# Half of the window-attention products on GpSimd, in chunks of 1024 elements, in a fused attention and expert kernel

## The chip, the cores and the metric

The kernel runs on one core of a Trainium2 chip. A core has five engines with queues of their own: TensorE (PE in the profile, its weight loads PEld), VectorE (DVE), ScalarE (ACT), GpSimd (POOL) and SyncE (SP). Each executes its queue strictly in the order in which the kernel was built, and engines wait for each other by semaphores. The metric is the time of one execution on the device in microseconds (us), as the median of several runs.

## The reference

The input x is 2 x 1024 rows of 256 numbers. Its rows are normalized (xn), and the result is the sum of three things:

```
x + attention(xn) + experts(xn)

attention: each row is 16 tokens of 16 channels; qkv = tok @ qkv_w
  two branches of 8 channels: windows of 8 tokens along one axis, then along the other
  softmax(q * 8**-0.5 @ k.T) @ v + depthwise 3x3 convolution of v within the window
  concatenate, project, layer norm, add to tok, transpose back
experts: 16 experts of 176 units, each row takes 6 of them, chosen in 2 of 4 groups
  sum over the 6 of weight * (silu(xn @ gate.T) * (xn @ up.T)) @ down.T, and one shared expert
```

The change concerns only the middle of the attention: for each window of 8 tokens and 8 channels, 8 x 8 scores as sums over 8 products q * k, and 8 x 8 outputs as sums over 8 products of a softmax weight and v.

## The kernel before, in words

The kernel first normalizes the rows, computes the shared expert, and sorts the rows by which experts they need. From about 108 us on, a long loop (lines 983 to 1015) does the routed experts on TensorE and lays the attention in between.

The expert work goes in slots: 96 of the kind "six" and 26 of the kind "extra", two to a pair. Per slot, `up` (line 827) makes a gate and an up product on TensorE (L831, four matmul records), ScalarE applies silu (L833), and VectorE multiplies gate, weight and up product to one hidden product (L834, `hms`; called h below). Per pair, TensorE transposes the hidden products (L845), ScalarE copies them out (L847), and TensorE multiplies by the down weights (L857, or L865 for extras). For extras VectorE adds each result to its tile (L920, called y); for sixes, once per tile of 128 rows (L912, called Y). A finished tile is added to the output by an indirect DMA that GpSimd issues (L926, "adds"). All rows of a tile were fetched by indirect DMAs of GpSimd (L802, "gathers") before.

The attention is done four times, for each half of the batch and each half of the columns, by `attention(b, h)` (line 642). One attention has 16 groups of windows, 8 for each branch, each with 8 windows' worth of work in the free dimension:

- `gather` and `project(i)`, i from 0 to 7: TensorE multiplies by the q, k and v weights (L660) and ScalarE copies q and k (L662, L663) and v (L664, L665) into place.
- `products(n)` and `scores(n)`, n from 0 to 12 in steps of NW = 4: VectorE multiplies 2048 elements on each of 128 partitions (L673) and sums them in eights (L677).
- `highest` (L683, L684, called X, and the exponential on ScalarE, L685) and `totals` (L688, L689, called S).
- `weighted(n)` and `values(n)`: the same with the weights and v (L694, L699).
- `divide` (L707, called D), and `transposed` back by TensorE (L714, L716).

The products of one chunk are in the room tagged "prod", 2048 elements per partition, which the next chunk takes again. After the four attentions, `attended` projects and normalizes the result, with some multiplies and adds on GpSimd (L782, L787), and GpSimd issues the DMAs that add it to the output (L954).

What sets the order: each step of the attention carries an estimated cost on VectorE and on TensorE, by hand. The loop over the slots adds up both and gives out the next attention step while VectorE's sum is below `pace` times TensorE's (line 1000), so that the steps are spread over the slots and end when 66 us of TensorE's work are left (`END`). The scheduler of the language then builds the queue of each engine from that, and may put a ready instruction ahead of one that it takes to be ready later.

Of the kernel before, what the change touches and what calls it, by code (L numbers as in the profile page):

```python
# [8 lines left out]
F32 = mybir.dt.float32  # L9
# [4 lines left out]
ALU = mybir.AluOpType  # L14
# [8 lines left out]
P = 128  # L23
B, H, W = 2, 1024, 256
C = 16
HD = 8
WIN = 8
NW = 4
E, I = 16, 176
LAST = I - P  # L30
HALF = P // 2
# [18 lines left out]
def csw_block_moe(ctx: ExitStack, tc: tile.TileContext, x, qkv_w, conv_w0, conv_b0, conv_w1, conv_b1,  # L50
# [19 lines left out]
    nc = tc.nc  # L70
# [3 lines left out]
    work = ctx.enter_context(tc.tile_pool(name="work", bufs=1))  # L74
# [74 lines left out]
    for c in range(16):  # L149
        n = sum(P // 2 if k % 2 == 0 else P for k in range(c)) + (((16 - c) * P - 1) / 2 if c % 2 == 0 else 0)  # L150
# [185 lines left out]
    full = [P, 16, E]  # L336
# [114 lines left out]
    for c in range(15, -1, -1):  # L451
        n = 16 - c
# [186 lines left out]

    oT = big.tile([P, 4, 2, 4, P], F32, name="oT", tag="oT")  # L640

    def attention(b, h):
        steps = []

        qk = work.tile([P, 2, 2, 8, WIN, HD], F32, tag="qk", name=f"qk{b}{h}")
        v = work.tile([P, 2, 8, HD, WIN], F32, tag="v", name=f"v{b}{h}")
        s = work.tile([P, 16, WIN, WIN], F32, tag="f1024", name=f"s{b}{h}", bufs=3)
        o = work.tile([P, 16, WIN, HD], F32, tag="f1024", name=f"o{b}{h}", bufs=3)
        sums = small.tile([P, 16, WIN], F32, name=f"sums{b}{h}", tag="sums")
        rows = work.tile([P, 8, P], F32, tag="f1024", name=f"rows{b}{h}", bufs=3)  # L650
        full = [P, NW, WIN, WIN, HD]

        def gather():
            for i in range(2):
                nc.scalar.copy(rows[:, 4 * i : 4 * i + 4].rearrange("p i (w r) -> p i w r", r=4),
                               xnT[:, h, :, 64 * b : 64 * b + 64].rearrange("p (i r) (w u) -> p u i w r", r=4, u=2)[:, i])

        def project(i):
            pq = ps_m.tile([P, 3, 8, C], F32, tag="m", name="pq")
            nc.tensor.matmul(pq.rearrange("p s t c -> p (s t c)"), lhsT=rows[:, i],  # L660
                             rhs=wq.rearrange("p s t c -> p (s t c)"), start=True, stop=True)
            nc.scalar.copy(qk[:, :, 0, i], pq[:, 0:2, :, 0:HD])  # L662
            nc.scalar.copy(qk[:, :, 1, :, i], pq[:, 0:2, :, HD:C])  # L663
            nc.scalar.copy(v[:, 0, i], pq[:, 2, :, 0:HD].rearrange("p t c -> p c t"))  # L664
            nc.scalar.copy(v[:, 1, :, :, i], pq[:, 2, :, HD:C])  # L665

        held = {}

        def products(n):
            pr = work.tile([P, NW, WIN, WIN, HD], F32, tag="prod", name="pr")  # L670
            br, m = n // 8, n % 8
            q_, k_ = (qk[:, part, br, m : m + NW] for part in range(2))
            nc.vector.tensor_tensor(pr, q_.unsqueeze(3).to_broadcast(full), k_.unsqueeze(2).to_broadcast(full), ALU.mult)  # L673
            held[n] = pr

        def scores(n):
            nc.vector.tensor_reduce(out=s[:, n : n + NW], in_=held.pop(n), axis=AX.X, op=ALU.add)  # L677

        rows_s = s.rearrange("p n q k -> p (n q) k")

        def highest():
            top = small.tile([P, P], F32, tag="top", name="top", bufs=1)
            nc.vector.tensor_reduce(out=top, in_=rows_s, axis=AX.X, op=ALU.max)  # L683
            nc.vector.tensor_tensor(rows_s, rows_s, top.unsqueeze(2).to_broadcast([P, P, WIN]), ALU.subtract)  # L684
            nc.scalar.activation(rows_s, rows_s, AF.Exp, scale=HD**-0.5)  # L685

        def totals():
            nc.vector.tensor_reduce(out=sums.rearrange("p n q -> p (n q)"), in_=rows_s, axis=AX.X, op=ALU.add)  # L688
            nc.vector.reciprocal(sums, sums)  # L689

        def weighted(n):
            pr = work.tile([P, NW, WIN, HD, WIN], F32, tag="prod", name="pv")
            br, m = n // 8, n % 8
            nc.vector.tensor_tensor(pr, s[:, n : n + NW].unsqueeze(3).to_broadcast(full),  # L694
                                    v[:, br, m : m + NW].unsqueeze(2).to_broadcast(full), ALU.mult)
            held[n] = pr

        def values(n):
            nc.vector.tensor_reduce(out=o[:, n : n + NW], in_=held.pop(n), axis=AX.X, op=ALU.add)  # L699

        def divide():
            xo = held["xo"] = work.tile([P, 8, 8, C], F32, tag="xo", name=f"xo{b}{h}")
            for br in range(2):
                to = xo[:, :, :, HD * br : HD * br + HD]
                if br:
                    to = to.rearrange("p i t c -> p t i c")
                nc.vector.tensor_tensor(to, o[:, 8 * br : 8 * br + 8],  # L707
                                        sums[:, 8 * br : 8 * br + 8, :].unsqueeze(3).to_broadcast([P, 8, WIN, HD]),
                                        ALU.mult)

        def transposed(i):
            po = ps_m.tile([P, 4, P], F32, tag="m", name="po")
            for j in range(4):
                nc.tensor.transpose(po[:, j, :], held["xo"][:, i + j].rearrange("p t c -> p (t c)"), ident)  # L714
            to = oT.rearrange("p g h r (b w i) -> p g h b i w r", b=B, i=2)[:, :, h, b, i // 4]
            nc.scalar.copy(to, po.rearrange("p j (w r) -> p j w r", r=4))  # L716


        steps.append((0.3, 0.0, gather))
        for i in range(8):  # L720
            steps.append((0.3, 0.65, lambda i=i: project(i)))
        for n in range(0, 16, NW):
            steps.append((2.3, 0.0, lambda n=n: products(n)))
            steps.append((2.3, 0.0, lambda n=n: scores(n)))
        steps.append((2.5, 0.0, highest))
        for n in range(0, 16, NW):
            steps.append((2.3, 0.0, lambda n=n: weighted(n)))
            if n == 0:
                steps.append((1.5, 0.0, totals))
            steps.append((2.3, 0.0, lambda n=n: values(n)))  # L730
        steps.append((1.4, 0.0, divide))
        for i in (0, 4):
            steps.append((0.3, 0.5, lambda i=i: transposed(i)))
        return steps

# [194 lines left out]
    att = []  # L930

    def all_steps():
        for steps in (extras_listed(), weights_prepared()):
            for _ in steps:
                yield 1.0, 0.1, lambda: None
        yield from attention_steps()

    def attention_steps():
        for b in range(B):
            for h in range(2):  # L940
                yield from attention(b, h)
        xe = []
        yield 0.6, 0.0, lambda: xe.extend(edges())
        att.extend(work.tile([P, 8, W], F32, tag=tag, name="att") for tag in ("prod", "qk"))
        for g in range(4):
            for h in range(2):
                yield 1.4, 3.9, lambda: attended(g, h, xe, att)
            if g % 2:
                waiting.extend([lambda m=m, b=b, n=g // 2: attention_added(m, b, n) for m in range(2) for b in range(B)])

    def attention_added(m, b, n):

        cols = slice(P * n, P * n + P)
        nc.gpsimd.dma_start(out=out[b, 512 * m : 512 * m + 512, cols].rearrange("(c p) d -> p c d", p=64),  # L954
                            in_=att[m][64 * b : 64 * b + 64, :, cols], accum_op=ALU.add)
# [2 lines left out]
    of_slot = {"six": (0.5, 2.0), "extra": (1.4, 2.25)}  # L958
    of_tile = (1.05, 0.25)
    END = 66  # L960
    in_walk = [11 * 1.0 + 4 * (16 * 2.3 + 3.3 + 2.5 + 1.5 + 1.4) + 0.6 + 8 * 1.4, 11 * 0.1 + 4 * 6.2 + 8 * 3.9]
    done = [0.0, 0.0]
    whole = [in_walk[n] + NTL * TOPK * of_slot["six"][n] + NX * of_slot["extra"][n] + NTL * of_tile[n] for n in range(2)]
    pace = (whole[0] - END * of_slot["six"][0] / of_slot["six"][1]) / (whole[1] - END)
# [18 lines left out]
    for u in range(len(laid_out) + 2):  # L983
        for q in range(2):
# [102 lines left out]
```

## Time and profile before

| what | value |
|---|---|
| median of 3 runs | 469.24 us (465.8 to 472.79) |
| the profiled execution | 463.79 us, its span 462.1 us |
| granted TensorE clock, mean | 0.987 |
| from 137.3 to 370.2 us | the four attentions, between pairs of expert slots |
| from 370.2 to 444 us | the rest of the expert slots with the end of the attention |
| from 444 to the end | the last tiles' adds to the output |

The four attentions, from the first product's start to the end of the last division, stand in VectorE's timeline at 137.32 to 185.73, 199.75 to 253.9, 266.61 to 315.1 and 321.39 to 370.2 us.

How to read the profile: a group's line has the source line, engine, operation, output and inputs with their shapes, the count, the busy time and the mean of one in ns, and then how long the engine was idle just before and what ended that. A timeline's line has start and duration in us, and in brackets the idle time ahead and what it waited for. A table of windows has start and end, length, and the busy time of each engine with its number of instructions.

### The profile page before, as it was taken

How to read it: one execution, taken by the hardware profiler on the slowest of the kernel's cores; microseconds unless marked ns; L12 is line 12 of the kernel's file. 1: busy time of each engine (PE TensorE's matmuls, PEld its weight loads, DVE VectorE, ACT ScalarE, POOL GpSimd, SP SyncE). 2: the span in 40 equal slices, each digit the busy share in tenths (PEclk: the TensorE clock that was granted, in tenths of full speed). 3: DMA queues.
4: the chain of work that ended last, by engine and by line, in shares of the span. 5: the costliest groups of instructions: out<-in, count | busy, mean ns of one | idle time of the engine just before them, and what ended most of it. 6: DMA issues, size and time to landing. Idle time of an engine off the chain costs nothing.

```text
span 462.1 us, 6437 instructions
## 1 busy us (share of the span) xinstructions
PE 412.7 (89%) x1726; PEld 258.8 (56%) x1727; DVE 304.3 (66%) x555; ACT 214.3 (46%) x510; POOL 108.4 (23%) x127
## 2 busy tenths in 40 slices
PE   0999999996999998999999999998998899999980
PEld 0436566463666665555556666665666545556760
DVE  5326956745729999469999199995999933333220
ACT  2936167222354463463632453626343147777220
POOL 7300000425400000000001312120221026766821
PEclk9999999998999999999999999999999999999996
DMA  8999960413310000100001221201013110185552
GB/s 234 325 287 279 260 211 2 106 39 86 96 31 21 24 27 24 28 5 27 20 24 35 47 41 35 43 24 27 23 35 84 35 17 19 48 123 99 75 72 23
DMA packets 38323, 35.39 MB, mean 77 GB/s; under 512 B 4112, under 2 KB 36208, under 8 KB 38256
## 3 DMA queue, kind: packets, MB, share of 16 engines
q1 hardware_dynamic: 28336, 23.28, 17.8%
q0 software_dynamic: 8896, 10.65, 14.3%
q10 hardware_dynamic: 1056, 1.05, 0.7%
q8 instruction: 16, 0.26, 0.2%
q14 instruction: 19, 0.16, 0.1%
HBM read 26.44 MB, written 10.62 MB: 80 GB/s over the span
## 4 chain that ended last, share of the span: by engine, by line
PE 39%; DVE 35%; issue 9%; ACT 7%; DMA 6%; DVEq 1%; POOL 1%; POOLq 0%; SPq 0%; ACTq 0%
PE pr_u L831 10%; DVE pr L673 6%; PE pp L766 6%; DVE s L677 6%; DVE pv L694 5%; DVE o L699 5%; PE pr_y L857 5%; DVE hms L834 4%; PE pg L270 3%; PE py L285 2%; PE pq L660 2%; DMA xg<-xw_d,of 2%; PE pu L270 2%; DMA xx<-in_x_dram 2%; PE plT L252 2%
## 5 line engine op out<-in xcount | busy, mean ns | idle before, releaser
L831 PE MATMUL pr_u<-w1s,xsT 128*128 x384 | 127.9, 464 | 0.7 <-DVE hms L834 0.4
L833 ACT ACTIVATE sg<-pr_u 128x176 f32<-128x176 f32 x122 | 38.6, 318 | 134.4 <-PE pr_u L831 107.4
L831 PEld LDWEIGHTS pr_u<-w1s,xsT 128*128 128x128 f32 x384 | 71.5, 191 | 35.9 <-issue 5.5
L926 POOL DMA_INDIRECT out_dram<-ysum,of x16 | 31.6, 1975 | 225.6 <-ACT sg L833 124.5
L834 DVE SCALAR_TENSOR_TENSOR hms<-sg,w,pr_u 128x176 f32<-128x176 f32 x96 | 36.8, 391 | 35.2 <-ACT sg L833 35.2
L673 DVE TENSOR_TENSOR pr<-qk 128x2048 f32<-128x2048 f32 x16 | 36.6, 2287 | 20.0 <-ACT qk L662 19.7
L845 PE MATMUL ph<-ident,hms 128*128 128x128 f32 x183 | 33.8, 280 | 8.7 <-DVE hms L834 7.3
L845 PEld LDWEIGHTS ph<-ident,hms 128*128 128x128 f32 x183 | 23.4, 142 | 29.7 <-DVE hms L834 13.2
L694 DVE TENSOR_TENSOR pv<-s,v 128x2048 f32<-128x2048 f32 x16 | 36.6, 2286 | 2.4 <-ACT s L685 2.4
L677 DVE TENSOR_REDUCE s<-pr 128x256 f32<-128x2048 f32 x16 | 36.5, 2278 | 0.0
L699 DVE TENSOR_REDUCE o<-pv 128x256 f32<-128x2048 f32 x16 | 36.3, 2268 | 0.0
L831 PE MATMUL pr_u<-w1s,xd 128*128 x104 | 33.5, 460 | 0.0
L847 ACT COPY hT<-ph 128x384 f32<-128x384 f32 x61 | 29.2, 478 | 3.1 <-PE ph L845 1.5
L857 PE MATMUL pr_y<-w2a,hT 128*128 x96 | 28.7, 380 | 0.0
L857 PE MATMUL pr_y<-w2b,hT 112*128 x96 | 28.7, 379 | 0.0
L857 PE MATMUL pr_y<-wts,hT 128*128 128x256 f32 x96 | 28.5, 379 | 0.0
L660 PE MATMUL pq<-wq,rows 128*128 128x384 f32 x64 | 24.7, 502 | 2.7 <-ACT oT L716 2.1
L285 PE MATMUL py<-room 128*128 128x256 f32 x96 | 23.9, 387 | 1.4 <-DVE room L279 1.4
L831 PEld LDWEIGHTS pr_u<-w1s,xd 128*128 128x128 f32 x104 | 19.6, 189 | 9.3 <-issue 0.4
L270 PE MATMUL pg<-xnT,room 128*128 128x512 f32 x48 | 24.1, 614 | 0.0
L270 PE MATMUL pu<-xnT,room 128*128 128x512 f32 x48 | 23.0, 602 | 0.0
L285 PEld LDWEIGHTS py<-room 128*128 128x128 f32 x96 | 17.4, 190 | 6.7 <-DVE room L279 2.5
(320 smaller groups left out, 635.3 us busy)
## 6 DMA issues: line engine op xcount, KB each, us to landing
w1s<-in_w_dram SPq DMA_DIRECT2D x22, 256.0 KB, 5.3
wts<-in_w_dram SPq DMA_DIRECT2D x61, 64.0 KB, 2.1
wts<-in_w_dram SPq DMA_DIRECT2D x61, 48.0 KB, 1.7
xw_d<-xx SPq DMA_DIRECT2D x4, 544.0 KB, 9.5
w2a<-in_w_dram SPq DMA_DIRECT2D x4, 512.0 KB, 10.5
out_dram<-ysh POOLq DMA_DIRECT2D x4, 512.0 KB, 5.5
xr<-xw_d POOLq DMA_DIRECT2D x4, 512.0 KB, 4.9
out_dram<-att POOLq DMA_DIRECT2D x8, 256.0 KB, 7.0
```

The costliest lines, as they stand in the source:

```text
L270: nc.tensor.matmul(ps, lhsT=w1h[:, half, h, P * m : P * m + P], rhs=xnT[:, h, 4 * k : 4 * k + 4, :].rearrange("p l q -> p (l q)"), start=( ...
L285: nc.tensor.matmul(py, lhsT=hms[k, m][:, P * c : P * c + P], rhs=w2h[:, m], start=(m == 0), stop=(m == 2))
L660: nc.tensor.matmul(pq.rearrange("p s t c -> p (s t c)"), lhsT=rows[:, i], rhs=wq.rearrange("p s t c -> p (s t c)"), start=True, stop=True)
L673: nc.vector.tensor_tensor(pr, q_.unsqueeze(3).to_broadcast(full), k_.unsqueeze(2).to_broadcast(full), ALU.mult)
L677: nc.vector.tensor_reduce(out=s[:, n : n + NW], in_=held.pop(n), axis=AX.X, op=ALU.add)
L694: nc.vector.tensor_tensor(pr, s[:, n : n + NW].unsqueeze(3).to_broadcast(full), v[:, br, m : m + NW].unsqueeze(2).to_broadcast(full), ALU. ...
L699: nc.vector.tensor_reduce(out=o[:, n : n + NW], in_=held.pop(n), axis=AX.X, op=ALU.add)
L831: nc.tensor.matmul(pu, lhsT=lhs[:, h, :], rhs=w1s[:, :, h, bass.ds(e * I, I)], start=(h == 0), stop=(h == 1))
L833: nc.scalar.activation(sg, pu[:, 0, :], AF.Silu)
L834: nc.vector.scalar_tensor_tensor(hm[:, 0:I], sg, w, pu[:, 1, :], op0=ALU.mult, op1=ALU.mult)
L845: nc.tensor.transpose(ph[:, s, :], units[:, P * s : P * s + P], ident)
L857: nc.tensor.matmul(py, lhsT=l_, rhs=r_, start=start and n == 0, stop=stop and n == 2)
```

## The change

Chunks have 2 groups of windows (NW = 2, 1024 elements), so there are eight chunks to the scores and eight to the values. The room for products is one tile of two halves that is kept for all four attentions. Chunks 1, 3, 5 and 7 are multiplied by GpSimd in the second half, the others by VectorE in the first; all sums stay on VectorE. GpSimd's first product is issued ahead of VectorE's first, and each later one right behind the sum that has read its half. `totals` comes ahead of all the weighted products. The estimated costs are 1.25 for each product of VectorE and each sum, nothing for a product of GpSimd; `in_walk`, from which `pace` follows, is made to match. One of the two tiles in which `attended` collects its result, which took the room of the products after the last attention, now is that kept tile.

```diff
-NW = 4
+NW = 2
...
+    prods_ = []
+    def multiplier(n):
+        return nc.gpsimd if n // NW % 2 else nc.vector
     def attention(b, h):
         steps = []
+        if not prods_:
+            prods_.append(work.tile([P, 2, NW, WIN, WIN, HD], F32, tag="prod", name="prods"))
+        prods = prods_[0]
...
         def products(n):
-            pr = work.tile([P, NW, WIN, WIN, HD], F32, tag="prod", name="pr")
+            pr = prods[:, n // NW % 2]
             br, m = n // 8, n % 8
             q_, k_ = (qk[:, part, br, m : m + NW] for part in range(2))
-            nc.vector.tensor_tensor(pr, q_.unsqueeze(3).to_broadcast(full), k_.unsqueeze(2).to_broadcast(full), ALU.mult)
+            multiplier(n).tensor_tensor(pr, q_.unsqueeze(3).to_broadcast(full), k_.unsqueeze(2).to_broadcast(full), ALU.mult)
...
         def weighted(n):
-            pr = work.tile([P, NW, WIN, HD, WIN], F32, tag="prod", name="pv")
+            pr = prods[:, n // NW % 2]
...
-            nc.vector.tensor_tensor(pr, s[:, n : n + NW].unsqueeze(3).to_broadcast(full),
+            multiplier(n).tensor_tensor(pr, s[:, n : n + NW].unsqueeze(3).to_broadcast(full),
...
-        for n in range(0, 16, NW):
-            steps.append((2.3, 0.0, lambda n=n: products(n)))
-            steps.append((2.3, 0.0, lambda n=n: scores(n)))
+        def in_turn(product, total):
+            steps.append((0.0, 0.0, lambda: product(NW)))
+            for n in range(0, 16, 2 * NW):
+                steps.append((1.25, 0.0, lambda n=n: product(n)))
+                steps.append((1.25, 0.0, lambda n=n: total(n)))
+                def last(n=n):
+                    total(n + NW)
+                    if n + 3 * NW < 16:
+                        product(n + 3 * NW)
+                steps.append((1.25, 0.0, last))
+        in_turn(products, scores)
         steps.append((2.5, 0.0, highest))
-        for n in range(0, 16, NW):
-            steps.append((2.3, 0.0, lambda n=n: weighted(n)))
-            if n == 0:
-                steps.append((1.5, 0.0, totals))
-            steps.append((2.3, 0.0, lambda n=n: values(n)))
+        steps.append((1.3 + 0.95, 0.0, totals))
+        in_turn(weighted, values)
...
-    in_walk = [11 * 1.0 + 4 * (16 * 2.3 + 3.3 + 2.5 + 1.5 + 1.4) + 0.6 + 8 * 1.4, 11 * 0.1 + 4 * 6.2 + 8 * 3.9]
+    in_walk = [11 * 1.0 + 4 * (24 * 1.25 + 3.3 + 2.5 + 2.25 + 1.4) + 0.6 + 8 * 1.4, 11 * 0.1 + 4 * 6.2 + 8 * 3.9]
```

The queue of VectorE as built, from the first attention's first product on, one letter for each instruction. P and W are products of VectorE (scores, values), T and V the sums of them, t and v the sums of GpSimd's products, X, S and D as above, h a hidden product, y and Y additions to a tile, e the edges and a the end of the attention; a bar stands behind each attention's last D and ahead of the next one's first P.

```
before
PThPhThPhThPhThXhXhWhShSVhWhhVhWhVhWhVhWhyVyhDhD | yyhhyyhhyy |
PhTPhyTyhhPyTyhhPyhThyXyXhyyWhhSVhyhyShWyVyhhWyVyhhWyhVhDD | hhhhYh |
PhTPhThPhThYPhThXhXhWhhSYSVhhWhVhWhVhYWhVhDD | hh |
PhTPhTYhPhThPhThhXYXhWhShSVhWhhYVhWhVhWhVhhDD |
YeeheeaaahaaaahaaahaaahaaaYhaaahaaahaahhhhYhhhhhhYhhY

after
PTtPhTtPhTthPthThXXhSWhhSVhvWhVhvWvhVhWvVhDhD | hhyyhhyyhhyyhhyyhhyy |
PThtPTPhytyThthPyTythXhyXySyShhyWhVhyvyWhVhvyWyVhvhyWyVhvhDyD | yhhhhhhYhhh |
PThtPTtPhThtYPthThXXhSWhhSVhvYWhVhvWvhVhWvhVDhD | Yhhhh |
PThtPTPhtYThthPtThXhXSWhhYShVhvWvhVhWvhVvhYWDhVhD |
eehhhhYeehaaaahaaahaaahaaahaaaYhaaahaaahaahhhhYhhhhhhYhhY
```

The queue of GpSimd after the change has, in this order: all 16 gathers; 16 products of the first two attentions; five adds; the third attention's four score products, an add, two weighted products, an add, two weighted products; an add; the fourth attention's three score products, an add, the fourth score product, a weighted product, an add and the fetch of the first rows for `attended` (L758), three weighted products; and then what was there before.

More of the change, by code (lines that the diff above doesn't have):

```diff
@@ L943, in attention_steps @@
         yield 0.6, 0.0, lambda: xe.extend(edges())
-        att.extend(work.tile([P, 8, W], F32, tag=tag, name="att") for tag in ("prod", "qk"))
+        att.extend([prods_[0].rearrange("p a w q k d -> p (a w q k d)").rearrange("p (n d) -> p n d", d=W),
+                                       work.tile([P, 8, W], F32, tag="qk", name="att")])
         for g in range(4):
```

## The prediction

> **What bounds the kernel now.** I read the busy shares first, then the stages as windows, then the groups by line, then the timeline of single instructions. TensorE leads the span, but TensorE's busy time is modelled from pipelined matmuls, so a stage has to say which engine ends last.
>
> ```profile
> PE 412.7 (89%) x1726; PEld 258.8 (56%) x1727; DVE 304.3 (66%) x555; ACT 214.3 (46%) x510; POOL 108.4 (23%) x127
> ```
>
> The windows of the third attention (266 to 314), the pause behind it, the fourth (321 to 370) and the tail of expert work; columns are window, length, and busy time of each engine with its instructions:
>
> ```profile
> core 0: us, PE busy (x) PEld busy (x) DVE busy (x) ACT busy (x) POOL busy (x), PEclk, DMA share, GB/s
> 266.00:314.00 48.00, 44.88 (x182) 30.65 (x180) 46.47 (x43) 19.84 (x58) 10.09 (x5) 1.00 0.20 38
> 314.00:321.00 7.00, 6.25 (x27) 4.20 (x28) 1.82 (x4) 4.75 (x16) 0.00 (x0) 1.00 0.09 22
> 321.00:370.00 49.00, 44.34 (x179) 30.10 (x177) 47.70 (x45) 18.00 (x54) 9.36 (x5) 1.00 0.19 43
> 421.00:444.00 23.00, 23.00 (x99) 16.66 (x98) 6.56 (x16) 9.63 (x23) 13.47 (x13) 1.00 0.69 110
> ```
>
> VectorE is full inside an attention (47.70 of 49) and almost idle between two (1.82 of 7), where TensorE is. The timeline of TensorE in the tail gives the price of expert work when nothing holds it: one pair of slots every 4.00 us, so 2.0 us per hidden product (h, L834).
>
> ```profile
> 425.35 2.53 PE L831 MATMUL pr_u<-w1s,xsT 128*128 x8
> 429.35 2.53 PE L831 MATMUL pr_u<-w1s,xsT 128*128 x8
> ```
>
> The prices on VectorE and GpSimd by line:
>
> ```profile
> L673 DVE TENSOR_TENSOR pr<-qk 128x2048 f32<-128x2048 f32 x16 | 36.6, 2287 | 20.0 <-ACT qk L662 19.7
> L677 DVE TENSOR_REDUCE s<-pr 128x256 f32<-128x2048 f32 x16 | 36.5, 2278 | 0.0
> L782 POOL TENSOR_TENSOR a<-a,lw 128x512 f32<-128x512 f32 x6 | 8.3, 1386 | 12.1 <-DVE a L781 12.1
> L787 POOL TENSOR_TENSOR att<-a,xr 128x256 f32<-128x256 f32 x12 | 12.6, 1074 | 5.3 <-DMA xr<-xw_d 5.0
> ```
>
> VectorE's timeline in the third attention: each instruction starts before the one ahead has drained, so what counts is start to start, 2.21 for a product (276.53 to 278.74) and 0.30 for an h.
>
> ```profile
> 276.53 2.28 DVE L673 TENSOR_TENSOR pr<-qk 128x2048 f32<-128x2048 f32 x1
> 278.74 0.39 DVE L834 SCALAR_TENSOR_TENSOR hms<-sg,w,pr_u 128x176 f32<-128x176 f32 x1
> 279.04 2.28 DVE L677 TENSOR_REDUCE s<-pr 128x256 f32<-128x2048 f32 x1
> 281.24 0.39 DVE L834 SCALAR_TENSOR_TENSOR hms<-sg,w,pr_u 128x176 f32<-128x176 f32 x1
> ```
>
> Last, the two engines side by side. The same descriptor work on GpSimd (L926) takes 1.55 us beside a reduction and 3.35 beside a two-input product:
>
> ```profile
> 295.30 1.55 POOL L926 DMA_INDIRECT out_dram<-ysum,of  x1 [9.72 <-DVE ysum L912]
> 295.80 2.23 DVE L699 TENSOR_REDUCE o<-pv 128x256 f32<-128x2048 f32 x1
> ...
> 308.91 2.28 DVE L694 TENSOR_TENSOR pv<-s,v 128x2048 f32<-128x2048 f32 x1
> 309.26 3.35 POOL L926 DMA_INDIRECT out_dram<-ysum,of  x1 [12.41 <-DVE ysum L912]
> ```
>
> 309.26 + 3.35 is 1.42 after the product's end at 311.19. It repeats at 282.23 (3.34 under L673), 331.69 (3.66 under L673) and 343.78 (2.28 under the 1.21 us L684), and never under a reduction (250.78, 269.36, 356.53: 1.54 to 1.65). So GpSimd stands still while VectorE has two inputs from this memory.
>
> **The change, part by part.** *VectorE's own work.* Removed: 32 products of 2048 and 32 sums of 2048. Added: 32 products and 64 sums of 1024. A 1024-element instruction costs 1.13 start to start (L683 at 341.97, next at 343.10; L684 at 343.43, next at 344.56). Per attention: before 8 x 2.21 + 8 x 2.2 = 35.3; after 24 x 1.13 = 27.1. Relief 8.2 per attention, 33 in all.
>
> *GpSimd's product.* No row has it. L782, 512 elements, takes 1.27 undisturbed (380.88, 386.89, 399.26; the 1.386 is a mean over disturbed ones). Upper end: L787's rate, 1.065 for 256 elements in runs of 8, gives 4.26. Lower end: the slope between L787 and L782, 1.27 + 2 x (1.27 - 1.065) = 1.68. I take 2.4, twice 1.27 less a fixed part of about 0.13 (from the memsets, 0.76 for 768 and 2.66 for 3072), because L782 is nearest: contiguous, one operand repeated. The Trainium skill, "GPSIMD Engine Reference", section 3.1, has 4497 ns for 2048 elements; half of that, 2.25, is an estimate that no run here shows, and by it the sum below would be about 4 us lower.
>
> *The new wait.* The second sum of each pair waits on GpSimd; behind it in VectorE's queue stand the next product and h's, and TensorE's transposes (L845) wait for the h's. One cycle, from one such sum's end to the next one's: VectorE's product goes at once and GpSimd needs 0.15 to see the freed half (L781 ends at 380.73, L782 starts at 380.88). If the rows of L926 hold for arithmetic, the two products exclude each other: 1.13 + 2.4 + 0.15 + 1.13 = 4.81. Where an h lies between, GpSimd is first and the VectorE product is the one that waits: 0.15 + 2.4 + 1.13 + 1.13 = 4.81 again. Before, the same four windows took 2.21 + 2.2 = 4.41, plus two h's. Ends for the exclusion: none at all, or this. I take this, since eight rows of L926 agree.
> The Trainium skill, "SBUF — State Buffer", section "Who interferes with whom", speaks against the change with the same rule for arithmetic: a VectorE instruction with two inputs in this memory and a GpSimd instruction that reads it exclude each other whole. The case's rows show it for descriptors only; by the page the sum is the one below, without the rule it would be rival 1.
>
> *One attention, first one, in its built order* (PTtPhTtPhTthPthTh XXhSWhhSVhvWhVhvWvhVhWvVhDhD). First product at 0; GpSimd's first at 2.0, since its windows' copies end 1.9 after the first two windows'; its sum ends at 4.55 + 1.13 = 5.7. Three cycles, 14.4. Then h, T, h: 1.75. X, X, h and the exponential: 3.4. Then GpSimd's first weighted product keeps VectorE's W off till 2.55; W, h, h, S, V, h, v: 5.2 more, 7.75. Three cycles, 14.4. V, h, D, h, D: 2.95. Sum 50.4; but it begins 1.9 earlier, as the product of two windows needs two projections and not four: 48.5. Before: 137.32 to 185.73, 48.4. So the relief of 8 is eaten by the waits: plus 0.1. The second attention comes out the same by the same steps (54.0 against 54.1). In the third and fourth, GpSimd's queue also holds adds (L926): one stands between two weighted products, 1.55 behind W; by the same steps plus 1.7 and plus 2.2. Together plus 4.
>
> *The h's that moved.* This is what costs. The built queue of VectorE has, from first product to last division, 20, 20, 19, 20 h's before and 15, 16, 15, 16 after; between attentions 4, 5, 2 before and 10, 9, 4 after; behind the last, 21 and 25. TensorE's order is nearly unchanged, and it puts those pairs ahead of the next projections. So attentions of the same length carry 17 fewer h's, TensorE idles there, and the h's are paid at TensorE's price where VectorE has nothing to do. First pause: five pairs of extras at 4.39 (186.95 to 191.34) in place of two and a part: plus 13. Second: 9 for 5 at 2.0, and a sum: plus 9. Third: plus 4.5 (two h's, and less prefetched). Tail: 4 at 2.0: plus 8. Together plus 34.5.
>
> *At nothing:* no DMA is added and SP's queue is as before. On GpSimd all 16 gathers (L802) precede the first product, as the last one issues at 125.31 and the first product at 137. The adds that now stand behind products were idle-waited by up to 19.1 us before; if that cover is gone each costs 1.55. Five early adds (20 us in a row) fit into the second pause, now some 21 us; without it the third attention's first GpSimd product is up to 4 late.
>
> Sum: 463.8 (the profiled execution; its span 462.1) + 4 + 34.5 = **502**. That execution lies 5.4 under the median of 469.24; I keep its base.
>
> **Rivals.**
> 1. *Exclusion holds for descriptors only.* For: no row has two arithmetic instructions side by side with two such inputs. Against: the instruction's operands, not its kind, should hold a port. A cycle is 0.15 + 2.4 + 0.15 + 1.13 = 3.83, near VectorE's own 3.39 and an h, and 0.98 less, 28 times: 502 - 28 = 474.
> 2. *GpSimd is never last (the other side: not slower).* Place: the wait of the second sum. It decides if the product lands inside VectorE's product and sum: 2.26 less the two 0.15, so at 1.96 or less, with nothing excluded; the 1.68 of the lower end would do. Then the first attention is VectorE's own work: 27.1, X 2.3, exponential 0.8, S 2.0, D 1.2, 15 h's 4.6, together 38.0 or 10.4 less than before; the others, likewise, 10.8, 9.9 and 9.6. That is 40.7 against 34.5: 463.8 - 6 = 458.
> 3. *GpSimd pays per short run, as L787 does.* For: the product's runs are 8 elements long. Against: L787's operands are strided by 16, the product's are not. 1.86 more for each of some 28 waiting cycles, 52: 554.
> That the change doesn't do what it says is out: the built queues have 32 products on GpSimd, each behind the sum that frees its half.
>
> **How the numbers follow.** Forecast 0.66; rival 1 0.13; rival 2 0.06; rival 3 0.10; else 0.05. Within the forecast the product's time moves the sum by 2.8 per 0.1 us (28 cycles), so 2.0 to 3.0 us is 491 to 519; the count of h's in the pauses is good to some 8. The range 470 to 526 takes rival 1 in at its foot and leaves out rivals 2 and 3. A measurement of this kernel tells about 2% from no change (459.9 and 478.6 around the median). Faster: half of rival 2, 0.03. Same: the rest of it and most of rival 1, 0.15. Slower 0.82.
>
> **What would show each step.** GpSimd's product group at 2.4 us, and longer by up to 1.13 where a VectorE product lies over it; a wait "sum from GpSimd" of about 1 us, some 28 times; VectorE's busy share in the attentions down to three quarters; attentions of 48 to 51 us; first and second pause near 27 and 21 us; tail 8 longer. Wrong if the products run side by side at full speed, if GpSimd's product is under 2.0 or over 3.0, or if the pauses don't grow.

## The result, and the profile after

The changed kernel is slower: a median of 496.95 us (494.29 to 498.91, four runs) against 467.69 us (465.8 to 472.79, four runs) for the kernel before, a ratio of 1.060 with a 95% interval of 1.050 to 1.071. Its profiled execution took 498.26 us with a span of 496.5, against 463.79 and 462.1.

The busy shares of the kernel after, and below them the TensorE clock that was granted in 40 slices of the span (in tenths, 9 is full speed):

```profile
PE 424.1 (85%) x1726; PEld 265.0 (53%) x1727; DVE 299.6 (60%) x587; ACT 213.9 (43%) x510; POOL 188.2 (38%) x159
...
PEclk9999999995999999998889998989989999999995
```

GpSimd (POOL) now does 32 products, but VectorE's busy time (DVE) has fallen by only 4.7 us from its 304.3. The prediction's own working promised a relief of 33 us there. Most of the rest is in the groups by line. The kernel after, products and sums on both engines (count, busy time, mean ns of one, then idle time ahead and what ended it):

```profile
L686 DVE TENSOR_REDUCE s<-prods 128x128 f32<-128x1024 f32 x32 | 38.8, 1214 | 10.9 <-POOL prods L682 10.7
L708 DVE TENSOR_REDUCE o<-prods 128x128 f32<-128x1024 f32 x32 | 38.5, 1206 | 8.3 <-POOL prods L703 8.3
...
L703 DVE TENSOR_TENSOR prods<-s,v 128x1024 f32<-128x1024 f32 x16 | 32.6, 2040 | 0.0
L682 DVE TENSOR_TENSOR prods<-qk 128x1024 f32<-128x1024 f32 x16 | 29.6, 1853 | 11.8 <-ACT qk L671 11.6
...
L682 POOL TENSOR_TENSOR prods<-qk 128x1024 f32<-128x1024 f32 x16 | 43.1, 2696 | 71.3 <-ACT qk L671 56.0 <-DVE s L686 12.5 <-ACT qk L672 2.8
L703 POOL TENSOR_TENSOR prods<-s,v 128x1024 f32<-128x1024 f32 x16 | 41.3, 2578 | 63.3 <-DVE o L708 35.0 <-ACT s L694 28.3
```

The sums take 1.21 us each, as a 1024-element reduction did before (L683, 1.21). VectorE's own products take 1.85 and 2.04 us on the mean, though they are of the same size. A product that nothing disturbs takes 1.22 (at 145.52 below), so 62.2 - 32 x 1.22 = 23.2 us of their busy time are ones in which they only stand. I call this **held**. To it come 19.0 us in which the sums **wait** for GpSimd (10.7 and 8.3). Held and wait, both on VectorE, are the two numbers that every experiment below is read by.

The first attention of the kernel after, on GpSimd's timeline and then on VectorE's, shows one product held by the other, from both sides:

```profile
141.99 2.36 POOL L682 TENSOR_TENSOR prods<-qk 128x1024 f32<-128x1024 f32 x1 [12.93 <-ACT qk L671]
145.75 3.20 POOL L682 TENSOR_TENSOR prods<-qk 128x1024 f32<-128x1024 f32 x1 [1.40 <-ACT qk L671]
...
154.88 2.36 POOL L682 TENSOR_TENSOR prods<-qk 128x1024 f32<-128x1024 f32 x1 [1.33 <-DVE s L686]
```

```profile
144.38 1.22 DVE L686 TENSOR_REDUCE s<-prods 128x128 f32<-128x1024 f32 x1 [1.70 <-POOL prods L682]
145.52 1.22 DVE L682 TENSOR_TENSOR prods<-qk 128x1024 f32<-128x1024 f32 x1
...
148.99 1.22 DVE L686 TENSOR_REDUCE s<-prods 128x128 f32<-128x1024 f32 x1 [0.81 <-POOL prods L682]
...
153.58 1.22 DVE L686 TENSOR_REDUCE s<-prods 128x128 f32<-128x1024 f32 x1 [0.80 <-POOL prods L682]
154.71 0.39 DVE L853 SCALAR_TENSOR_TENSOR hms<-sg,w,pr_u 128x176 f32<-128x176 f32 x1
155.02 3.30 DVE L682 TENSOR_TENSOR prods<-qk 128x1024 f32<-128x1024 f32 x1
```

At 145.52 VectorE is first: it runs in 1.22, and GpSimd's product, begun at 145.75, takes 3.20 in place of 2.36. At 154.88 GpSimd is first, because an h (L853) lies ahead of VectorE's product: now GpSimd runs in 2.36 and VectorE's product takes 3.30 in place of 1.22. Either way one cycle of a pair lasts the same: sums that waited start at 144.38, 148.99 and 153.58, so 4.61 and 4.59.

The windows of the first attention, the pause behind it, the third attention, the next pause and the fourth attention in the kernel after (columns as in the tables of the prediction):

```profile
core 0: us, PE busy (x) PEld busy (x) DVE busy (x) ACT busy (x) POOL busy (x), PEclk, DMA share, GB/s
140.00:189.00 49.00, 38.85 (x154) 26.12 (x155) 41.85 (x46) 21.48 (x65) 22.35 (x8) 1.00 0.07 20
189.00:212.00 23.00, 22.31 (x100) 13.97 (x99) 8.04 (x20) 11.06 (x30) 0.00 (x0) 1.00 0.09 26
287.00:337.00 50.00, 41.02 (x150) 27.37 (x149) 43.87 (x47) 18.11 (x54) 26.94 (x11) 0.93 0.13 27
337.00:347.00 10.00, 9.31 (x43) 6.50 (x41) 2.50 (x7) 5.31 (x15) 1.57 (x1) 1.00 0.19 36
347.00:398.00 51.00, 41.90 (x159) 27.59 (x158) 44.16 (x51) 16.99 (x54) 28.01 (x13) 0.97 0.17 37
```

The attentions last at least as long as before, but TensorE stands in them: busy for 41.02 of 50 us in the third, where it was busy for 44.88 of 48, and with 150 matmuls for 182. The expert work that no longer fits is in the pauses: the first is 23 us long, TensorE is full in it (22.31), and VectorE has 8 us of work.

In numbers, by VectorE's timeline (an attention reaches from the start of its first product to the end of its last division, and the tail from there to the end of the span). Both kernels were profiled again later on (e11, e12 and e13 below), so the means are over three executions and two:

| part | before, three executions | after, two | difference of means |
|---|---|---|---|
| start of the first attention | 137.3, 137.3, 139.7 | 140.2, 139.1 | +1.5 |
| attentions 1 to 4 | 48.5, 54.2 to 54.9, 48.6, 48.9 | 48.8, 55.8, 50.7, 51.2 | +6.0 |
| pauses 1 to 3 | 13.9 to 15.6, 12.4 to 12.7, 6.2 | 23.3, 18.1, 9.2 | +17.2 |
| tail | 91.8 to 93.3 | 98.6 | +6.0 |
| span | 462.1, 463.5, 467.6 | 496.5, 494.0 | +30.8 |

### The profile page after: what moved, and what is told of

It reads as the page before. It is cut to its first block, busy times and chain, and to the rows that moved or that the text cites. A ratio compares the mean times of both kernels' runs of the same rounds, so it can differ in the third digit from the quotient of the medians.

```text
span 496.5 us, 6510 instructions
## 1 busy us (share of the span) xinstructions
PE 424.1 (85%) x1726; PEld 265.0 (53%) x1727; DVE 299.6 (60%) x587; ACT 213.9 (43%) x510; POOL 188.2 (38%) x159
## 5 line engine op out<-in xcount | busy, mean ns | idle before, releaser
L850 PE MATMUL pr_u<-w1s,xsT 128*128 x384 | 134.3, 479 | 15.3 <-DVE hms L853 15.2
L682 POOL TENSOR_TENSOR prods<-qk 128x1024 f32<-128x1024 f32 x16 | 43.1, 2696 | 71.3 <-ACT qk L671 56.0
L853 DVE SCALAR_TENSOR_TENSOR hms<-sg,w,pr_u 128x176 f32<-128x176 f32 x96 | 36.8, 389 | 51.7 <-ACT sg L852 51.7
L703 POOL TENSOR_TENSOR prods<-s,v 128x1024 f32<-128x1024 f32 x16 | 41.3, 2578 | 63.3 <-DVE o L708 35.0
L945 POOL DMA_INDIRECT out_dram<-ysum,of x16 | 27.7, 1729 | 50.0 <-DVE ysum L931 16.8
L686 DVE TENSOR_REDUCE s<-prods 128x128 f32<-128x1024 f32 x32 | 38.8, 1214 | 10.9 <-POOL prods L682 10.7
L708 DVE TENSOR_REDUCE o<-prods 128x128 f32<-128x1024 f32 x32 | 38.5, 1206 | 8.3 <-POOL prods L703 8.3
L850 PE MATMUL pr_u<-w1s,xd 128*128 x104 | 35.5, 479 | 3.9 <-DVE hms L853 3.9
L682 DVE TENSOR_TENSOR prods<-qk 128x1024 f32<-128x1024 f32 x16 | 29.6, 1853 | 11.8 <-ACT qk L671 11.6
L703 DVE TENSOR_TENSOR prods<-s,v 128x1024 f32<-128x1024 f32 x16 | 32.6, 2040 | 0.0
L876 PE MATMUL pr_y<-w2b,hT 112*128 x96 | 28.9, 382 | 0.0
L288 POOL DMA_DIRECT2D out_dram<-ysh x4 | 3.7, 929 | 63.7 <-ACT ysh L286 63.7
L669 PE MATMUL pq<-wq,rows 128*128 128x384 f32 x64 | 24.7, 502 | 2.8 <-ACT oT L725 2.1
```

The costliest lines, as they stand in the source:

```text
L682: multiplier(n).tensor_tensor(pr, q_.unsqueeze(3).to_broadcast(full), k_.unsqueeze(2).to_broadcast(full), ALU.mult)
L703: multiplier(n).tensor_tensor(pr, s[:, n : n + NW].unsqueeze(3).to_broadcast(full), v[:, br, m : m + NW].unsqueeze(2).to_broadcast(full), ...
L850: nc.tensor.matmul(pu, lhsT=lhs[:, h, :], rhs=w1s[:, :, h, bass.ds(e * I, I)], start=(h == 0), stop=(h == 1))
L853: nc.vector.scalar_tensor_tensor(hm[:, 0:I], sg, w, pu[:, 1, :], op0=ALU.mult, op1=ALU.mult)
L876: nc.tensor.matmul(py, lhsT=l_, rhs=r_, start=start and n == 0, stop=stop and n == 2)
L945: nc.gpsimd.indirect_dma_start(out=out_rows, out_offset=bass.IndirectOffsetOnAxis(ap=of[:, t : t + 1], axis=0), in_=ysum[:, t, :], in_offs ...
```

## The experiments

The theory: a GpSimd product and a VectorE product with two inputs exclude each other, so the attentions gain nothing from the second engine, and the h's that the new order puts outside them are paid in the pauses and the tail. The rivals: chunking alone costs it (e1), GpSimd's slowness alone costs it, with no exclusion (e2, e3), or the waits alone are the price and the order of the h's is not (e5). Every kernel below is the kernel after with the edit shown.

**e1: all products on VectorE, in chunks of 1024.**

```diff
-        return nc.gpsimd if n // NW % 2 else nc.vector
+        return nc.vector
```

> All products back on VectorE, in the same 1024-element chunks, the same two halves, the same steps and estimated costs as in the changed kernel; GpSimd multiplies nothing. Theory (waits on GpSimd behind mutual exclusion, plus hidden products that moved out of the attentions): no waits, and VectorE's queue again has 18 to 20 h's in each attention, so about the time of before plus 4 us for the fixed part of 64 more instructions on VectorE: 468 to 475 us, no long pauses. Rival (the smaller chunks, the new order of the steps or the lower pace cost the time, not GpSimd): 485 us or more.

Measured: 467.08 us beside 466.82 for the kernel before, ratio 1.001 (0.997 to 1.005), a little under the range expected. VectorE's products in this kernel:

```profile
L682 DVE TENSOR_TENSOR prods<-qk 128x1024 f32<-128x1024 f32 x32 | 38.1, 1219 | 7.9 <-ACT qk L671 7.9
```

1.219 us for each, nothing held. So the smaller chunks, the split room and the rewritten loops cost nothing that can be measured; all of the loss comes with GpSimd.

**e2: VectorE's share made by an instruction with one input.** GpSimd's products stay. VectorE's products are replaced by a reduction over one element, which has the same size and one input, so the scores are not those of the reference; the order of VectorE's queue is the same.

```diff
-            multiplier(n).tensor_tensor(pr, q_..., k_..., ALU.mult)
+            if n // NW % 2:
+                nc.gpsimd.tensor_tensor(pr, q_..., k_..., ALU.mult)
+            else:
+                one_operand(pr, k_)   # tensor_reduce, out and in 128x1024
```

> VectorE's half of the products is replaced by an instruction of the same size that reads one operand only (a reduction over one element, so VectorE's share is not multiplied); GpSimd's half, the waits and the order of VectorE's queue stay exactly as in the changed kernel. Theory (two-input instructions of VectorE and GpSimd exclude each other whole): GpSimd's product takes 2.36 us every time, VectorE's stand-in never more than 1.25 us, a cycle falls from 4.6 to about 3.8 us, 28 times 0.8: 472 to 478 us. Rival (GpSimd is merely slow and the overlap is harmless): the cycle stays at 4.6 and the time at 494 to 499 us.

Measured: 470.46 us, ratio 1.007 (1.004 to 1.010), 1.5 us under the range expected. The tile view of the products' room in this kernel (shortest, median and longest of 16, in ns):

```profile
L650 DVE TENSOR_REDUCE prods<-qk x16: 1209/1214/1221, 139.8 to 337.8; 128x1024 f32<-128x1024 f32 x16
L687 POOL TENSOR_TENSOR prods<-qk x16: 2338/2358/2764, 141.6 to 337.7; 128x1024 f32<-128x1024 f32 x16
L711 POOL TENSOR_TENSOR prods<-s,v x16: 2346/2357/2371, 161.7 to 361.5; 128x1024 f32<-128x1024 f32 x16
```

GpSimd's products are back at a median of 2.36, and VectorE's stand-ins at 1.21, though they overlap in time as before. The order of the queues is the same, so the exclusion is shown, and it is worth 26.5 us. The rival that GpSimd is merely slow falls for that part.

The edit takes away the second input and changes the operation with it. Which of the two matters can be seen in the kernel after, where an addition to a tile (y) is the same operation as the products but has only one input from this memory (`pr_y` is the matmul's output). It runs inside a product of GpSimd, and neither is longer than alone:

```profile
260.26 2.35 POOL L703 TENSOR_TENSOR prods<-s,v 128x1024 f32<-128x1024 f32 x1 [4.05 <-DVE o L708]
260.41 0.41 DVE L939 TENSOR_TENSOR ysum<-ysum,pr_y 128x256 f32 x1
```

**e3: GpSimd multiplies half of its chunk** (512 of 1024 elements; the room is zeroed once, so half of every second chunk's terms are left out).

```diff
+                half = [P, 1, WIN, WIN, HD]
+                nc.gpsimd.tensor_tensor(pr[:, 0:1], q_[:, 0:1]..., k_[:, 0:1]..., ALU.mult)
```

> GpSimd multiplies only 512 of the 1024 elements of its chunks (the other half of its room is zero, so these products are left out); VectorE's work and nearly its queue stay. Theory (waits and moved hidden products): GpSimd's product takes 1.27 us, the waits are nearly gone, cycle 3.6 to 3.8 us, but the pauses between the attentions stay at 20 and 18 us: 463 to 472 us, although VectorE has 33 us less to do than before the change. Rival (only the waits cost; where the hidden products stand is harmless): without waits the relief comes through until TensorE is the bound, 435 to 445 us.

Measured: 469.33 us, ratio 1.006 (1.003 to 1.010), in the range expected. GpSimd's products now take 1.42 and 1.49 us on the mean (median 1.27, as expected). The rival, 435 to 445, falls: with most of the waits gone, held at 8.7 and wait at 5.1, the attentions shrink to 40.7, 49.6, 43.0 and 43.2, and still the kernel is no faster than before. The pauses stay at 23.4, 20.7 and 9.3 and the tail at 98.7. This is the price of the moved h's by itself.

**e4: a third room, so that GpSimd's product is begun a whole pair ahead.**

```diff
+        third = xo.rearrange(...)   # the output's tile, free until the division
+        rooms = [prods[:, 0], prods[:, 1], prods[:, 0], third]
-            pr = prods[:, n // NW % 2]
+            pr = rooms[n // NW % 4]
-                    if n + 3 * NW < 16:
-                        product(n + 3 * NW)
+                    if n + 5 * NW < 16:
+                        product(n + 5 * NW)
```

> The whole computation, with a third room of 1024 elements (the tile that the attention's result takes later), so that GpSimd's products have two rooms in turn and each is begun one cycle earlier, behind the sum before the last; VectorE's queue is letter for letter that of the changed kernel. Theory: GpSimd has a whole cycle for 1.13 of exclusion and 2.36 of work, VectorE's waits nearly vanish (under 15 us busy and idle together in place of some 45), attentions of 40 to 43 us, pauses and tail as in the changed kernel: 463 to 472 us. Rival (GpSimd's products are simply too slow beside VectorE's, whenever they begin): 485 us or more.

Measured: 480.70 us, ratio 1.028 (1.022 to 1.034). This missed both ranges. The sums wait less, 7.8 us in place of 19.0, but the products do not stop excluding each other because one starts earlier. The timeline of both engines in this kernel:

```profile
240.97 2.35 POOL L707 TENSOR_TENSOR prods<-s,v 128x1024 f32<-128x1024 f32 x1 [4.37 <-DVE o L712]
241.14 3.26 DVE L707 TENSOR_TENSOR prods<-s,v 128x1024 f32<-128x1024 f32 x1
```

GpSimd is first by 0.17 us, and VectorE's product stands for 2 us. Held is still 15.7 us. The expectation had counted the waits of the sums alone; the wait inside the product is as dear, and the profile shows it only as a longer duration.

**e5: the h's pinned.** Each step of the attention is bound to be issued behind the h of two slots ago, so that the scheduler can't move the h's out of the attention. The rooms are as in the kernel after.

```diff
-                step[2]()
+                with tc.issue_after(hidden_[max(0, len(hidden_) - 1 - 2)]):
+                    step[2]()
```

> The changed kernel, with one thing more: each attention step's VectorE instructions are queued behind the hidden product (h) emitted two slots earlier, so that VectorE's queue has 22, 22, 17 and 17 h's in the four attentions (15, 16, 15, 16 in the changed kernel) and 3, 3, 2 in the pauses (10, 9, 4). GpSimd's products, their two halves and the exclusion stay. Theory (the h's that moved into the pauses are a price of their own): VectorE's waits now hide h's, the pauses fall from 51 us together to some 30, the attentions grow by 0 to 3 us each: 476 to 486 us. Rival (only the waits on GpSimd cost; where the h's stand is harmless): 494 us or more.

Measured: 486.41 us beside 468.56, ratio 1.039 (1.031 to 1.047), 0.4 us over the range expected. The pauses fell from 50.7 us to 22.0 in all, further than the expected 30: 22, 22, 17 and 17 h's are now inside the attentions, for 15, 16, 15 and 16. But the attentions grew by 21 us, where 0 to 3 each had been expected. About half of that is in one group of this kernel:

```profile
L703 DVE TENSOR_TENSOR prods<-s,v 128x1024 f32<-128x1024 f32 x16 | 41.5, 2594 | 0.0
```

2.594 us in place of 2.040: an h ahead of VectorE's product lets GpSimd go first, and then it is VectorE that stands. Held grew from 23.2 to 33.1. Of the rest, 16 more h's at 0.30 from start to start are 5 us, and in VectorE's timeline h's in the attentions now wait 4.2 us for ScalarE's silu. So the h's and the exclusion are not two prices to be added: the one sets the other.

**e7: GpSimd's product behind VectorE's.** The three rooms of e4, and each GpSimd product waits until the VectorE product ahead of it has ended. It then runs beside the sums and h's, which read at most one input from this memory (an h's other large input comes from the matmul's output).

```diff
+            def first(n):
+                mine = product(n)
+                if n + 3 * NW < 16:
+                    other = product(n + 3 * NW)
+                    tc.add_manual_dep(other.ins, mine.ins.name, ...)
```

> The three rooms, but each GpSimd product of the next cycle is begun behind VectorE's product of this cycle (a wait of GpSimd on VectorE) and runs beside the sums, which have one input; VectorE's queue is letter for letter that of the changed kernel. Theory (exclusion is what is left in the three-room kernel, where VectorE's own products were held for 16 us and its sums for 8): VectorE's products are held under 5 us in all, sums wait under 8, attentions 41 to 45 us, pauses as in the changed kernel: 466 to 473 us. Rival (the third room's remainder is GpSimd being late, not exclusion): 478 us or more, since GpSimd now begins later than in the three-room kernel.

Measured: 472.50 us, ratio 1.009 (1.006 to 1.011), in the range expected, though held was to be under 5 us and is 7.7 (15.7 in e4). One more wait, and 8.2 us less than e4.

**e8: e7 with the h's pinned as in e5.**

```diff
+                with tc.issue_after(hidden_[max(0, len(hidden_) - 1 - 2)]):
+                    step[2]()
```

> Both together: three rooms, GpSimd's products behind VectorE's, and the hidden products pinned as in the pinned kernel. Theory: attentions of 43 to 50 us that carry 17 to 22 h's, pauses of 30 us together, tail some 97 us: 448 to 460 us, faster than both kernels. Rival (TensorE's work or the clock bounds the whole, and the relief of VectorE can't come through): 463 us or more.

Measured: 457.97 us beside 468.56, ratio 0.976 (0.969 to 0.984), in the range expected. Pinning, which gained 10.5 us on two rooms, gains 14.5 here. VectorE's products with the values in this kernel (those of the scores still take 1.43 on the mean), and one pair in its timeline:

```profile
L708 DVE TENSOR_TENSOR prods<-s,v 128x1024 f32<-128x1024 f32 x16 | 20.4, 1272 | 0.0
```

```profile
289.07 1.22 DVE L708 TENSOR_TENSOR prods<-s,v 128x1024 f32<-128x1024 f32 x1
290.43 2.37 POOL L708 TENSOR_TENSOR xo<-s,v 128x1024 f32<-128x1024 f32 x1 [1.56 <-DVE prods L708]
```

VectorE's product ends at 290.29, GpSimd's begins 0.14 later and takes 2.37: both at their undisturbed time.

**e9: e1 with the h's pinned** (all on VectorE), to see what the order alone brings.

```diff
+                with tc.issue_after(hidden_[max(0, len(hidden_) - 1 - 2)]):
+                    step[2]()
```

> All products on VectorE in chunks of 1024, and the hidden products pinned as in the pinned kernel; GpSimd multiplies nothing. It asks whether the pinned order alone made the 458 us of the kernel with GpSimd behind VectorE. Theory: VectorE has its 33 us back and is full in the attentions, so the order of the h's can gain little: 463 to 470 us, like the all-VectorE kernel's 467. Rival (the order was the gain, GpSimd's share is worth nothing): 456 to 461 us.

Measured: 463.34 us beside 467.34, ratio 0.988 (0.980 to 0.995), in the range expected. About 4 us are the order's, with no GpSimd. All four executions of e8 (456.56 to 458.79) are shorter than all four of this kernel (460.2 to 466.99), so in e8 GpSimd's share is worth some 5 to 7 us beside that.

**e10: e8, each step behind the h of one slot ago.**

```diff
-                with tc.issue_after(hidden_[max(0, len(hidden_) - 1 - 2)]):
+                with tc.issue_after(hidden_[max(0, len(hidden_) - 1 - 1)]):
```

> GpSimd's products behind VectorE's, three rooms, and the h's pinned one slot earlier, which gives 23, 23, 17, 18 h's in the attentions, 2, 2, 2 in the pauses and 23 behind. Theory: nearly nothing left to move, 454 to 459 us. Rival (the tighter pin makes VectorE wait for h's that TensorE has not fed yet): 462 us or more.

Measured: 454.02 us beside 467.34, ratio 0.970 (0.963 to 0.976), in the range expected and the best of all. The windows of its first and third attention:

```profile
139.00:192.00 53.00, 52.95 (x223) 36.26 (x223) 43.88 (x61) 27.76 (x82) 19.63 (x8) 1.00 0.10 26
...
263.00:309.00 46.00, 44.73 (x181) 30.17 (x180) 41.84 (x52) 20.09 (x60) 26.00 (x11) 0.99 0.16 32
```

TensorE is full in both (52.95 of 53 and 44.73 of 46, for 41.02 of 50 in the kernel after), and VectorE is below it. The attention now hides behind the expert work, which I take to bound this stage, since TensorE has little idle time left there. No run has all products on VectorE with this lag, so how the 13 us of e10 divide between the order and GpSimd is not shown.

**e11, e12, e13: the kernel before twice more and the kernel after once**, unchanged, for the start of the first attention, which in the first two profiles differs by 2.9 us.

> The kernel before, unchanged, profiled once more. In the changed kernel's profile the first product starts 2.9 us later than in the profile of before (140.2 against 137.3), and in all other kernels built so far at 138.2 to 140.7. Theory: this is a difference between executions (how long a fetch of rows takes and what clock TensorE is granted afterwards), not between kernels: then this one starts between 138 and 141, with a span of 463 to 466. Rival: the build of the changed kernels does it: then this one starts at 137.0 to 137.6, with a span of 461.5 to 463.

> The same once more: by the theory (a difference between executions) a start that differs from that of the other profile of the same kernel by up to 3 us and lies in 137 to 141; by the rival (a difference between builds) again 137.0 to 137.6.

> The changed kernel, unchanged, profiled once more. Theory (the later start is a difference between executions): it starts anywhere from 137 to 141, and its first attention, pauses and tail repeat within 1 us. Rival (a difference between builds): again 139.9 to 140.5.

Measured: starts at 137.25, 139.72 and 139.07 us. The first product of the kernel before in e12:

```profile
139.72 2.29 DVE L673 TENSOR_TENSOR pr<-qk 128x2048 f32<-128x2048 f32 x1 [4.20 <-ACT qk L662]
```

The same kernel thus starts 2.4 us later in another execution, and the kernel after 1.1 earlier than at first. e11 alone speaks for the rival, e12 and e13 against it. At least half of the 2.9 us is a difference between executions. What differs between the kernels shows in the timelines, and pulls both ways. From the first projection (L660, L669) to the first product it takes 3.52 to 3.53 us in all three executions of before and 1.79 in both of after. But TensorE starts that projection later: at 133.8, 133.7 and 136.2 us before, at 138.4 and 137.3 after. Ahead of it stands one more slot's gate and up product (52 matmul records for 48), and its longest wait for gathered rows is 3.39 to 3.63 us in all eleven profiles of changed kernels, where it is 2.00 to 2.10 in the three of before. So a part of the later start belongs to the changed order ahead of the attention; how large it is beside the scatter of executions stays open. The attentions and pauses of the kernel after repeat within 0.6 us.

**All together.** Held and wait from the groups, the attentions, pauses and tail from VectorE's timeline, us of one profiled execution each:

| kernel | span | held | wait | four attentions | three pauses | tail |
|---|---|---|---|---|---|---|
| before | 462.1 | 0 | 0 | 200.2 | 32.8 | 91.8 |
| after | 496.5 | 23.2 | 19.0 | 206.7 | 50.7 | 98.8 |
| e1 all VectorE | 465.2 | 0 | 0 | 203.2 | 27.7 | 94.4 |
| e2 one input | 468.6 | 0 | 16.3 | 179.8 | 50.2 | 98.8 |
| e3 half | 467.6 | 8.7 | 5.1 | 176.5 | 53.4 | 98.7 |
| e4 three rooms | 479.7 | 15.7 | 7.8 | 187.6 | 53.6 | 98.5 |
| e5 pinned | 484.0 | 33.1 | 17.1 | 227.7 | 22.0 | 95.0 |
| e7 behind | 472.3 | 7.7 | 7.8 | 182.8 | 51.0 | 100.3 |
| e8 behind, pinned | 456.6 | 4.2 | 8.9 | 196.4 | 23.1 | 97.8 |
| e9 VectorE, pinned | 465.3 | 0 | 0 | 209.1 | 18.5 | 96.9 |
| e10 behind, lag 1 | 453.3 | 3.2 | 13.9 | 202.7 | 16.4 | 95.2 |

Read down the unpinned kernels with GpSimd: against the kernel after, e2 has 25.9 us less of held and wait, e3 28.4, e4 18.7 and e7 26.7, and their spans are 27.9, 28.9, 16.8 and 24.2 shorter. Held plus wait accounts for nearly all of what they differ in. And none of them falls below before, because in them pauses and tail together stay 24 to 28 us above those of before.

## Why the prediction was right

Direction and size came out as forecast: 502 predicted, 496.95 measured. Its steps in turn:

- **GpSimd's product, 2.4 us:** 2.36 undisturbed, median 2.36 over 16. Right.
- **The exclusion:** this was the disputed step, taken from eight rows of descriptor work. It holds for arithmetic, from both sides (3.20 and 3.30 us above), and e2 takes it away. Rival 1 is out.
- **The cycle, 4.81:** measured 4.61 and 4.59, from two small terms. The signal was mis-sized: GpSimd's product ends at 148.95 and the sum starts at 148.99, 0.04 us and not some 0.15. And GpSimd's product ends 3.43 us after VectorE's starts (145.52 to 148.95), where the prediction had 1.13 + 2.4 = 3.53.
- **The attentions together, +4 with a start 1.9 us earlier.** By the table's cut, where the earlier start lengthens the attention and shortens the pause before it, the prediction had attentions of 50.5, 55.9, 52.2 and 53.0, so +11.4; measured were +6.0 in the means. Oversized by 5, mostly for the cycle: 0.2 less, some 28 times.
- **The wait, "about 1 us, some 28 times":** the shape was wrong. There are 15 waits for GpSimd (10 of the first kind, 5 of the second; the longest 1.7 and 2.2 us), 19.0 us in all, because the other half of the price sits within VectorE's own products as held time. The sum came close: 42.2 us of held and wait in 32 pairs are 1.32 a pair, against 4.81 less VectorE's own 3.39, so 1.42.
- **VectorE's busy share in the attentions, three quarters:** missed as the profile shows it, for the same reason. It is 41.85 of 49, 43.87 of 50 and 44.16 of 51 us, 0.85 to 0.88, because held time counts as busy. Less the held time of these attentions (3.8, 5.8 and 5.0) it is 0.76 to 0.78.
- **The moved h's, +34.5.** By the same cut the prediction had +20.8 in the pauses and +8 in the tail; measured were +17.2 and +6.0. First and second pause were to be near 27 and 21, by this cut 25 and 19, and are 23.3 and 18.2. The mechanism was right: e3 pays it alone, and e5, e8 and e10 take it away. The size was between 5 and 6 too large. The counts of h's are those of the timelines but for the last, 20 and 24 behind the last attention and not 21 and 25, with the same difference of 4; the first line of the queue drawn for before has one W, one V and two h's too many. That the two prices can be added is not general: in e5 the moved h's came back at the price of more held time.
- **Five early adds fit into the second pause:** they did. The third attention's first GpSimd product starts at 288.61 us, 0.79 us after the engine came free, and waits for ScalarE's copy of q and k, not for the adds.
- **The start:** forecast 1.9 earlier, since the first product needs two projections only. That step holds: from the first projection to the first product it takes 1.79 us instead of 3.52, so 1.7 less. The waits for ScalarE's copies ahead of later attentions shrank too (from 5.13, 4.81 and 5.57 us to 3.25, 2.95 and 4.56). What was put at nothing is TensorE's work ahead of the first projection, which starts 3.3 us later in the means (e11 to e13 above), so the first attention starts 1.5 us later and not 1.9 earlier.

Against the means the sum came out 7.6 us too large (5.4 in the attentions and 5.6 in pauses and tail, less 3.4 at the start). Against the median it is 5 us, because the one execution that the sum was based on has a span 2.3 us under the mean of three. So part of the closeness is luck: the late start and the low base each took back some of what the other terms were too large by.

The Trainium skill, "SBUF — State Buffer", section "Who interferes with whom", says that a VectorE instruction with two inputs in this memory and a GpSimd instruction that reads it shut each other out, and that the order of issue decides which one is blocked. The runs agree in both parts: 3.20 us on GpSimd when VectorE was first, 3.30 on VectorE when GpSimd was, and 2.36 and 1.21 in e2, where VectorE had one input.

What stays open is how much the lower granted clock costs. It was 0.953 and 0.957 in the two executions of the kernel after and 0.987, 0.984 and 0.975 in three of the kernel before, and no run separates it from the idle time of TensorE that comes with it. In e2 the mean clock says little about the time: executions at 0.979 and 0.965 took 470.40 and 470.50 us.

## What to carry to other kernels

Before giving work to a second engine, look for rows where the two already run side by side, and compare durations there: an exclusion shows as a longer instruction, not as a wait. If they exclude each other, start the slower engine's instruction right behind the instruction that shuts it out, so that it runs beside those that do not (e7: 24 us less than the kernel after, 16 of them from the third room that e4 has too). And look at what a new order puts elsewhere: a stage may get the relief it was promised and hand its filler work to the next stage, so pin the filler and only then judge the change (e10, 3.0% faster than before, where the change as made was 6.0% slower).

## What the runs showed of the hardware

- Order alone moves what the exclusion costs: the same 1024-element product took 1.22 us on VectorE undisturbed, 2.04 on the mean in the kernel after, and 2.59 in e5, where only the h's places had changed.
- The signal between the engines is not the same both ways: in the kernel after, VectorE's end to GpSimd's start took 0.07 to 0.17 us (0.08 at 154.80 to 154.88, 0.15 at 145.60 to 145.75), and GpSimd's end to VectorE's start 0.03 to 0.04 (148.95 to 148.99).
- GpSimd multiplies 1024 elements in runs of 8, one operand repeated, in 2.36 us: no dearer per element than the 512 contiguous ones of before (1.27 us, so 2.54 for twice as many). At 512 elements (e3) its median is the same 1.27.
